# Layer 3 of a fused graph-attention kernel: the order of scores, products and small tasks rewritten in bursts of ten

## The chip, the core and the metric

The kernel runs on one core of a Trainium2 chip. The metric is the device time of one execution in microseconds (us); three runs of the kernel before had a median of 2003.11 us, from 2002.91 to 2005.37. The engines are called PE (matrix products; PEld are its weight loads), DVE (vector), ACT (activation functions), POOL and SP (which issues DMAs). Each engine works through its own instructions in order; PSUM holds what PE writes.

## What is computed

Four layers of graph attention over 16 batches (B) of 1024 nodes (N) with 64 features, all with one adjacency matrix of 1024 x 1024; after each, x becomes the layer norm of x plus the layer's output. The change touches layer 3, which is, cut to what matters:

```python
mask = graph + eye(N) > 0
h = einsum('bnc,hdc->bhnd', x, Wh)                    # 4 heads of 64
out_h = softmax(where(mask, h @ h.T, NEG)) @ h + bh   # per head
z = leaky_relu(concat_heads(out_h), 0.2)              # 256 features
h2 = einsum('bnk,dk->bnd', z, Wo)
out2 = softmax(where(mask, h2 @ h2.T, NEG)) @ h2 + bo
z2 = leaky_relu(out2, 0.2)
x = layernorm(x + layernorm(z2) * gamma + beta)
```

## The kernel before

Layers 0 to 2 end at about 650 us; the rest of the time is layer 3. It works in units. A **head unit** takes one pair of heads (n = 0, 1), one of 8 chunks k of 128 nodes and one half (h) of the other nodes: `scores` (L1332) multiplies 64-row tiles of hT into a score slot of two PSUM banks and has ACT take the exponential into a buffer e (L1340); `mask` multiplies e by the adjacency aT on DVE (L1344); `product` (L1347) multiplies e by vals in 64-column tiles and accumulates over k (L1351). A float32 product stands in the profile as two passes, so a unit has four PE rows for its scores and four for its product. A batch has 32 head units and 8 **outer units** for the second attention (L1479, L1484, L1497, L1504), which run one batch later; their masks cost DVE one more pass, which adds up the row sums (L1489).

Score slots come from `ps_s`, a ring of three (tag "s"). The small tasks that need PSUM take their slots from the same ring, through `two_banks` and `one_bank` (L680 to L690): the next one waits until the third before it has been read. The accumulators `acc0` and `acc1` take the other two banks; before, the two halves of heads alternate between them or share one. The buffers e are a ring of 11, from which z and the adjacency chunks are taken as well.

The small tasks of a batch are: `prep_x` (transposes x, pxT), `prep_h` (phT, copied to hT by ACT), `prep_sq` (squares, hsq), `shift_of` (column norms pn on PE, a maximum on DVE, a maximum over partitions on POOL, and later the shift on ACT), `prep_v` (vals); then for each pair of heads `project_T` (poT), `inverse` (the reciprocal of the row sums, which goes out to DRAM and comes back as r) and `quotient`; then `h_2T` (ph2T), `h_2v` (ph2v), and after the outer units `gather` (po2) and ten steps of layer norms, most on DVE.

The order is written out by hand. `run(plan)` (L1950 on) goes through 8 **bursts** a batch of five, five, five, five, three, three, three and three head units, with two outer units put into each of the last four. A burst issues all its scores; then the tasks listed under `mids`; then the products of the burst before (`drain`); then its own masks; then the tasks listed under `slots`. The engines PE, ACT, DVE and POOL keep that order. So PE alternates between five scores (64 rows by 128 columns of the array, 64*128 in the profile) and five products (128*64), with mids between them.

Of the kernel before, what the change touches and what calls it, by code (L numbers as in the profile page):

```python
# [582 lines left out]
def fast_path(  # L583
# [669 lines left out]
    def nodes_adj(c):  # L1253
        a_sb = l3.tile([P, N], I32, tag="e", name=f"adj3_{c}", bufs=11)
        nc.sync.dma_start(a_sb, adj_v[c])

        def convert():
            nc.vector.tensor_scalar(
                aN[:, c, :].rearrange("p (k q) -> p k q", q=P), a_sb.rearrange("p (q k) -> p k q", k=C),
                0.0, None, ALU.is_gt,  # L1260
            )
            own = aN[:, c, c * P : (c + 1) * P]
            nc.vector.tensor_tensor(own, own, ident16, ALU.max)

        return convert
    xT2, hTs, shifts, vals, zs, zTs = {}, {}, {}, {}, {}, {}

    def shift_of(key, sq):
# [3 lines left out]
        for c in range(n):  # L1272
            nc.tensor.matmul(
                pn[:, 2 * c : 2 * c + 2], sq[:, c * P : (c + 1) * P], pair_ones, start=True, stop=True
            )
        top = small.tile([P, 1], F32, tag="top", name="top")
        nc.vector.tensor_reduce(top, pn[:, : 2 * n], AX.X, ALU.max)  # L1277
# [49 lines left out]
    def heads(b, n):  # L1327
        held = {}

        def scores(k, h):  # L1330
# [8 lines left out]
            e = l3.tile([P, 2, HALF], F32, tag="e", name="e", bufs=11)  # L1339
# [7 lines left out]
        def product(k, h, e):  # L1347
            if k == 0:
                held[h] = ps_h.tile([P, HALF], F32, tag=f"acc{h * (1 - n)}", name=f"y_{b}_{n}_{h}")
# [49 lines left out]
        def project(q):  # L1399

            if q == 0:
                zs[b] = l3.tile([P, C, P], F32, tag="e", name=f"z_{b}", bufs=11)
# [30 lines left out]
    BURSTS, LAST = 8, 5  # L1433

    def prep_out(b):
# [7 lines left out]
        def h_2T():  # L1443
# [13 lines left out]
            nc.scalar.activation(sq, hT[:, 0, :], AF.Square)  # L1457
            nc.vector.tensor_copy(hT[:D, 1, :], hT[D:, 0, :])
# [10 lines left out]
        return z_T, h_2T, h_2v  # L1469

    def head_out(b):
        held = {}

        def scores(k):
# [8 lines left out]
            e = l3.tile([P, 2, HALF], F32, tag="e", name="e", bufs=11)  # L1483
# [357 lines left out]
    slots, mids = {}, {}  # L1841
# [4 lines left out]
    def at(b, j, task, where=slots):  # L1846
        where.setdefault((b, j), []).append(task)

    for c in range(C):
        convert = {}  # L1850
        at(0, c, lambda c=c, convert=convert: convert.update(go=nodes_adj(c)))
        at((c + 1) // BURSTS, (c + 1) % BURSTS, lambda convert=convert: convert["go"]())
    for b in range(B):
        z_T, h_2T, h_2v = outs[b][0]
        chain = [
            *work[b][0][1], *work[b][1][1], *([z_T] if b == E else []), h_2T,
            lambda b=b: shift_of(b, hTs[b][1]), h_2v,
        ]
        ends = outs[b][1][1]

        places = [(5, mids), (5, mids), (5, slots), (9, mids), (9, mids), (9, slots), (10, mids), (11, mids), (12, mids)]
        places += [(18, mids), *((j, slots) for j in (18, 19, 19, 20, 22, 24, 24, 24, 25, 28))]
        if b == E - 2:
            places[9:] = [(17, mids), *((j, slots) for j in (17, 17, 18, 18, 20, 20, 21, 22, 22, 24))]
        elif b == E - 1:
            places[9:] = [(j, slots) for j in (15, 15, 15, 15, 15, 17, 17, 17, 18, 18)]
        elif b == E:
            places[3] = 7, mids
            places[4:] = [(j, slots) for j in [7] * 5 + [10] * 11]
        for task, (j, where) in zip(chain + ends, places):  # L1870
            t = min(j // BURSTS, E - b)
            at(b + t, j - t * BURSTS, task, where)


    ended = slots[E, BURSTS - 1]
    slots[E, BURSTS - 1] = [ended[i] for i in (5, 0, 1, 6, 2, 3, 7, 8, 9, 4)]
    rest = slots[E, BURSTS + 2]
    slots[E, BURSTS + 2] = [*rest[2:4], rest[0], *rest[4:7], rest[1], *rest[7:]]
# [166 lines left out]
```

## Time and profile before

| | |
|---|---|
| median of three runs | 2003.11 us |
| the profiled execution | 2005.96 us |
| its span, first to last instruction | 2003.7 us |
| granted PE clock, mean | 0.981 |
| first score of layer 3 | 650.0 us |
| first score of batch 4, of batch 14 | 959.4, 1772.7 us |
| last score (outer units of batch 15) | 1969.0 us |

The page of the profile lists per engine busy time, share of the span and number of instructions; then groups of instructions with the source line, engine, operation, what is written and read, shapes, count, busy time, mean length, and the idle time before them with who ended it. A timeline lists start, length and group in order of time. In a span of consecutive batches the pattern repeats every two batches, since preparation is done for two batches at once.

### The profile page before, as it was taken

What the parts mean: (1) busy time and instruction counts of PE and PEld (TensorE: products, weight loads), DVE (VectorE), ACT (ScalarE), POOL (GpSimd) and SP (SyncE); (2) the same over time, 40 slices, a digit from 0 to 9 for tenths busy, and PEclk for the clock granted to TensorE, in tenths of its full rate; (3) what the DMA queues carried; (4) which work ended last, traced back from release to release, by engine and by line L of the source; (5) the groups of instructions that cost most, each with busy time, mean ns of one, the idle gap of its engine ahead of it and who ended that gap; (6) DMA issues with size and microseconds to landing.
All of it is one profiled execution on the core that took longest, in us unless ns stands there. A gap on an engine that the chain in (4) does not pass through costs nothing.

```text
span 2003.7 us, 25793 instructions
## 1 busy us (share of the span) xinstructions
PE 1891.7 (94%) x9545; PEld 768.3 (38%) x9545; DVE 1764.4 (88%) x2930; ACT 1333.4 (67%) x2343; POOL 81.9 (4%) x77
## 2 busy tenths in 40 slices
PE   7999989998888999999999999999999999999985
PEld 3444447763332333333333333333333333333322
DVE  5899988879999868798898899989989899889996
ACT  5356567767776766676767766766677676776543
POOL 0000000000000000000000000000000000000001
PEclk8999989999999999999999999999999999999997
DMA  7000000000000210000000000000000000100000
GB/s 175 1 1 1 1 1 1 1 1 1 1 1 11 66 31 12 12 22 17 12 17 27 12 17 12 20 26 12 17 12 27 17 12 17 28 12 17 11 17 18
DMA packets 45603, 35.89 MB, mean 18 GB/s; under 512 B 37279, under 2 KB 37344, under 8 KB 45470
## 3 DMA queue, kind: packets, MB, share of 16 engines
q1 hardware_dynamic: 45166, 34.14, 6.6%
q8 instruction: 77, 1.26, 0.3%
q14 instruction: 56, 0.46, 0.1%
q10 hardware_dynamic: 304, 0.03, 0.0%
HBM read 29.45 MB, written 4.70 MB: 17 GB/s over the span
## 4 chain that ended last, share of the span: by engine, by line
PE 61%; DVE 24%; ACT 11%; issue 3%; DMA 1%; POOL 0%; SPq 0%; POOLq 0%; DVEq 0%; ACTq 0%
PE y L1351 16%; PE s L1336 14%; DVE e L1344 8%; DVE e L991 7%; PE y_l L1003 6%; PE po L1776 5%; ACT e L1340 5%; PE y L1504 4%; PE u_l L1015 3%; PE s L1479 3%; ACT e L1484 2%; PE ph2T L1452 1%; PE phT L1310 1%; PE poT L1378 1%; ACT x L780 1%
## 5 line engine op out<-in xcount | busy, mean ns | idle before, releaser
L1340 ACT ACTIVATE e<-s,shift 128x1024 f32<-128x1024 f32 x512 | 542.6, 1119 | 320.1 <-PE s L1336 320.0
L1344 DVE TENSOR_TENSOR e<-e,aT 128x1024 f32<-128x1024 f32 x512 | 599.0, 1215 | 14.8 <-ACT e L1340 14.6
L1351 PE MATMUL y<-e,vals 128*64 128x512 f32 x2048 | 494.0, 605 | 12.5 <-ACT yT L1358 5.9
L1336 PE MATMUL s<-hT 64*128 64x512 f32 x2048 | 497.3, 605 | 1.4 <-ACT e L1340 0.9
L991 DVE SCALAR_TENSOR_TENSOR e<-G_l,q,aT 128x1024 f32<-128x1024 f32 x256 | 315.3, 1275 | 3.9 <-ACT G_l L968 3.9
L1336 PEld LDWEIGHTS s<-hT 64*128 64x128 f32 x2048 | 186.3, 186 | 290.4 <-issue 153.3
L1003 PE MATMUL y_l<-e,vals_l 128*64 128x512 f32 x1024 | 254.2, 616 | 26.9 <-DVE e L991 20.1
L1351 PEld LDWEIGHTS y<-e,vals 128*64 128x64 f32 x2048 | 135.9, 137 | 303.8 <-issue 205.0
L1497 DVE TENSOR_TENSOR e<-e,aT 128x1024 f32<-128x1024 f32 x128 | 156.3, 1225 | 10.4 <-ACT e L1484 1.0
L1489 DVE SCALAR_TENSOR_TENSOR junk<-e,aN 128x1024 bf16<-128x1024 f32 x120 | 146.1, 1217 | 0.0
L1484 ACT ACTIVATE e<-s,shift 128x1024 f32<-128x1024 f32 x128 | 142.0, 1116 | 0.2 <-PE s L1479 0.2
L1504 PE MATMUL y<-e,h2v 128*64 128x512 f32 x512 | 131.6, 597 | 0.6 <-DVE e L1497 0.6
L1479 PE MATMUL s<-h2T 64*128 64x512 f32 x512 | 130.7, 591 | 0.0
L1003 PEld LDWEIGHTS y_l<-e,vals_l 128*64 128x64 f32 x1024 | 62.3, 138 | 160.4 <-issue 75.7
L1776 PE MATMUL po<-hi,aR 128*128 128x512 f32 x256 | 102.7, 402 | 11.2 <-ACT hi L1705 7.3
L1279 POOL PARTITION_ALL_REDUCE gtop<-top x48 | 55.1, 1148 | 1302.0 <-DVE top L1277 996.5
L1776 PE MATMUL po<-lo,aR 128*128 128x512 f32 x256 | 101.1, 396 | 0.0
L780 ACT ACTIVATE x<-m,bn_shift,bn_rstd 128x64 f32<-128x64 f32 x256 | 88.5, 430 | 0.0
L1479 PEld LDWEIGHTS s<-h2T 64*128 64x128 f32 x512 | 49.9, 186 | 60.0 <-issue 26.2
L1383 ACT COPY zT<-poT 64x512 f32<-64x512 f32 x124 | 71.9, 580 | 1.3 <-PE poT L1378 0.2
L1504 PEld LDWEIGHTS y<-e,h2v 128*64 128x64 f32 x512 | 36.5, 137 | 76.0 <-issue 54.0
L978 ACT ACTIVATE vals_l<-x,p 128x64 f32<-128x64 f32 (+1 forms) x256 | 64.3, 339 | 0.0
(252 smaller groups left out, 1874.9 us busy)
## 6 DMA issues: line engine op xcount, KB each, us to landing
r<-inverse SPq DMA_DIRECT2D x62, 256.0 KB
adj<-in_adj_dram SPq DMA_DIRECT2D x16, 512.0 KB
x<-in_x_dram SPq DMA_DIRECT2D x16, 256.0 KB
out_dram<-res SPq DMA_DIRECT2D x16, 256.0 KB
rows<-yT SPq DMA_DIRECT2D x62, 4.0 KB
sums<-rows SPq DMA_DIRECT2D x31, 8.0 KB
inverse<-rt SPq DMA_DIRECT2D x31, 8.0 KB
wl<-in_L_gnn_Wh_dram SPq DMA_DIRECT2D x2, 64.0 KB
```

The costliest lines, as they stand in the source:

```text
L991: nc.vector.scalar_tensor_tensor(e, G[b - b % 2][:, b % 2, :], pq[b - b % 2][1][:, k, b % 2 : b % 2 + 1], aT[:, k, :], ALU.max, ALU.mult,)
L1003: nc.tensor.matmul(held["y"][h * D : (h + 1) * D, :], vals[b][:, k, :], e[:, h * HALF : (h + 1) * HALF], start=(k == 0), stop=(k == C - 1),)
L1336: nc.tensor.matmul(s[:, i, :], hT[rows, k * P : (k + 1) * P], hT[rows, cols], start=True, stop=True)
L1340: nc.scalar.activation(e, s, AF.Exp, bias=shifts[b, n])
L1344: nc.vector.tensor_tensor(e, e, bc_mid(aT[:, k, h * HALF : (h + 1) * HALF], 2), ALU.mult)
L1351: nc.tensor.matmul(held[h][i * D : (i + 1) * D, :], vals[b][:, k, :], e[:, i, :], start=(k == 0), stop=(k == C - 1),)
L1479: nc.tensor.matmul(s[:, i, :], hT[rows, (i + k // CH) % 2, k % CH * P : (k % CH + 1) * P], hT[rows, 0, :], start=True, stop=True,)
L1484: nc.scalar.activation(e, s, AF.Exp, bias=shifts[b])
L1489: nc.vector.scalar_tensor_tensor(junk.rearrange("p c q -> p (c q)").bitcast(BF16), e.rearrange("p i q -> p (i q)"), 1.0, aN[:, k, :], ALU. ...
L1497: nc.vector.tensor_tensor(e, e, aT[:, k, :].rearrange("p (i q) -> p i q", i=2), ALU.mult)
L1504: nc.tensor.matmul(held["o"][h * D : (h + 1) * D, :], vals["out", b][:, k, :], e[:, h, :], start=(k == 0), stop=(k == C - 1),)
L1776: nc.tensor.matmul(po.rearrange("p q k f -> p (q k f)"), aR[:, k, ic * P : (ic + 1) * P], e[:, k].rearrange("p q k f -> p (q k f)"), start ...
```

## The change

It reorders layer 3; what is computed stays. The order of the built program's instructions shows the following.

- A batch has 4 bursts (Q) of eight head units, one (n, h) each, and two outer units after them, of an earlier batch. Scores are issued in the order heads, outer; masks likewise.
- Products are issued in the same burst, after the MID tasks, and the last two (KEPT, the outer units') stay back until the products of the next burst. So PE issues ten scores, MID tasks, two kept products, eight head products, END tasks. From the seventh burst on, the PE order repeats every eight bursts: `8+2 scores, poT, 10 products, ph2v, phT` / `scores, pn, pn, po2, products, phT` / `scores, poT, products, phT` / `scores, pn, pn, ph2T, products, pn` / `scores, poT, products, ph2v` / `scores, pxT, po2, products` / `scores, poT, products` / `scores, ph2T, products, pn, phT`.
- Tasks have three places in a burst, TOP (before the scores), MID (after the masks of the first six units; PE's part stands after all the scores) and END, with an order number. `phT` and `ph2v` stand at END, between products and scores; `poT` and `ph2T` at MID. Two `hsq` tasks per two batches stand at TOP, ahead of the exponentials of that burst.
- Deferred steps (`catch_up`: shifts, and steps of the roots) come after the first four scores and at the burst's end.
- `shift_of` for the outer attention copies the norms from PSUM with ACT first; `h_2T`'s two copies on DVE become a task of their own, `swap`.
- Head products always accumulate in `acc0`. The ring e has 12 buffers; z uses the buffer of xT, the adjacency chunks the buffer of zT, two chunks of 512 KB at a time, four times, each loaded after the conversion of the ones before.
- The last batch has two bursts of the usual kind and three of eight with outer units mixed in, then the outer units of batch 15 in 5 and 3 as before.

The diff, cut to its core:

```diff
-        a_sb = l3.tile([P, N], I32, tag="e", name=f"adj3_{c}", bufs=11)
-        nc.sync.dma_start(a_sb, adj_v[c])
-
-        def convert():
+        a_sb = l3.tile([P, 2, N], I32, tag="zT", name=f"adj3_{c}", bufs=1)
+        for i in range(2):
+            nc.sync.dma_start(a_sb[:, i, :], adj_v[c + i])
...
+        norms = pn[:, : 2 * n]
+        if copied:
+            norms = small.tile([P, 2 * n], F32, tag="norms", name="norms", bufs=1)
+            nc.scalar.copy(norms, pn[:, : 2 * n])
         top = small.tile([P, 1], F32, tag="top", name="top")
-        nc.vector.tensor_reduce(top, pn[:, : 2 * n], AX.X, ALU.max)
+        nc.vector.tensor_reduce(top, norms, AX.X, ALU.max)
...
-            e = l3.tile([P, 2, HALF], F32, tag="e", name="e", bufs=11)
+            e = l3.tile([P, 2, HALF], F32, tag="e", name="e", bufs=12)
...
-                held[h] = ps_h.tile([P, HALF], F32, tag=f"acc{h * (1 - n)}", name=f"y_{b}_{n}_{h}")
+                held[h] = ps_h.tile([P, HALF], F32, tag="acc0", name=f"y_{b}_{n}_{h}")
...
-                zs[b] = l3.tile([P, C, P], F32, tag="e", name=f"z_{b}", bufs=11)
+                zs[b] = l3a.tile([P, C, P], F32, tag="xT", name=f"z_{b}", bufs=1)
...
-    BURSTS, LAST = 8, 5
+    Q, KEPT, LAST = 4, 2, 5
...
+    TOP, MID, END = range(3)
+
+    def at(burst, place, task, order=5):
+        table.setdefault((burst, place), []).append((order, len(table.get((burst, place), [])), task))
+
+    for c in range(0, C, 2):
+        convert = []
+        load, go = [(0, TOP), (0, MID), (0, END), (1, MID)][c // 2], [(0, MID), (0, END), (1, MID), (1, END)][c // 2]
+        at(*load, lambda c=c, convert=convert: convert.extend(nodes_adj(c)), 6)
+        for i in range(2):
+            at(*go, lambda i=i, convert=convert: convert[i](), 4)
...
+        places = ((2, MID, 3), (2, MID, 4), (2, END, 5)) if b < E else ((2, END, 3), (3, TOP, 4), (3, END, 5))
+        for task, (j, place, order) in zip(first, places):
+            at(g + j, place, task, order)
...
+                [*second, h_2T, swap, lambda b=b: shift_of(b, hTs[b][1], True), h_2v],
+                ((4, MID, 3), (4, MID, 4), (4, END, 5), (5, MID, 8), (5, END, 1), (5, END, 2), (6, MID if b == E - 1 else END, 8)),
...
+            (11, MID), (11, END), (11, END), (12, TOP), (12, TOP), (13, TOP), (13, TOP), (13, MID), (14, TOP), (14, TOP),
+            (15, TOP),
...
+            (-5, MID, 0, lambda b=b: prep_x(b)),
+            (-3, END, 9, lambda b=b: prep_h(b, 0, 0)), (-2, MID, 6, lambda b=b: prep_sq(b, 0, 0)),
+            (-2, END, 9, lambda b=b: prep_h(b, 0, 1)), (-1, TOP, 6, lambda b=b: prep_sq(b, 0, 1)),
+            (-2, END, 6, lambda b=b: prep_v(b)),
+            (-1, MID, 0, lambda b=b: shift_of((b, 0), hTs[b, 0][1])),
+            (-1, MID, 0, lambda b=b: shift_of((b + 1, 0), hTs[b + 1, 0][1])),
+            (-1, END, 9, lambda b=b: prep_h(b, 1, 0)), (0, MID, 6, lambda b=b: prep_sq(b, 1, 0)),
+            (0, END, 9, lambda b=b: prep_h(b, 1, 1)), (1, TOP, 6, lambda b=b: prep_sq(b, 1, 1)),
+            (1, MID, 0, lambda b=b: shift_of((b, 1), hTs[b, 1][1])),
+            (1, MID, 0, lambda b=b: shift_of((b + 1, 1), hTs[b + 1, 1][1])),
+            (2, END, 6, lambda b=b: prep_v(b + 1)),
...
-        for j in range(BURSTS):
-            n = 5 if j < 4 else 3
-            burst, units = units[:n], units[n:]
-            if j >= 4:
-                for i, unit in enumerate(outer[2 * (j - 4) : 2 * (j - 3)]):
-                    burst.insert(1 + 2 * i, unit)
-            plan.append((b, j, burst))
+        for q in range(Q if b < E else 2):
+            outer = outs[(Q * b + q - 6) // Q][1][0] if Q * b + q >= 6 else []
+            o = (Q * b + q - 6) % Q * 2
+            burst = units[q * C : (q + 1) * C] + outer[o : o + 2]
+            if (b, q) == (E, 1):
+                burst = [burst[i] for i in (0, 1, 2, 3, 8, 4, 5, 9, 6, 7)]
+            plan.append((burst, 4, KEPT if len(burst) > C else 0))
+    heads_last, outer_last = work[E][1][0][:], outs[E - 1][1][0][:]
+    for kinds, kept in (("hhhhohho", KEPT), ("ohhohhho", KEPT), ("hohohohh", 0)):
+        plan.append(([(heads_last if kind == "h" else outer_last).pop(0) for kind in kinds], 4, kept))
...
-        for b, j, burst in plan:
+        for burst, (units, soonest, kept) in enumerate(plan):
+            tasks(burst, TOP)
+            if burst == 0:
+                catch_up()
+            made = []
+            for i, unit in enumerate(units):
+                if i == soonest:
+                    catch_up()
+                made.append((unit, unit[0]()))
+
+            def masked(some):
+                for (_, mask, product), e in some:
+                    mask(e)
+                    waiting.append(lambda product=product, e=e: product(e))
+
+            cut = min(6, len(units))
+            masked(made[:cut])
+            if soonest >= len(units):
+                catch_up()
+            tasks(burst, MID)
+            masked(made[cut:])
+            while len(waiting) > kept:
+                waiting.pop(0)()
             catch_up()
-            made = [(unit, unit[0]()) for unit in burst]
-            tasks(mids, b, j)
-            while roots:
-                roots.pop(0)()
-            drain()
-            made = [(product, mask(e)) for (_, mask, product), e in made]
-            waiting.extend(lambda product=product, e=e: product(e) for product, e in made)
-            if (b, j, burst) == plan[-1]:
-                drain()
-            tasks(slots, b, j)
+            tasks(burst, END)
```

## The prediction, on record before the change was run

> **What bounds the kernel now.** I read the page's first part, then its costliest groups.
>
> ```profile
> PE 1891.7 (94%) x9545; PEld 768.3 (38%) x9545; DVE 1764.4 (88%) x2930; ACT 1333.4 (67%) x2343; POOL 81.9 (4%) x77
> ...
> L1340 ACT ACTIVATE e<-s,shift 128x1024 f32<-128x1024 f32 x512 | 542.6, 1119 | 320.1 <-PE s L1336 320.0
> L1344 DVE TENSOR_TENSOR e<-e,aT 128x1024 f32<-128x1024 f32 x512 | 599.0, 1215 | 14.8 <-ACT e L1340 14.6
> L1351 PE MATMUL y<-e,vals 128*64 128x512 f32 x2048 | 494.0, 605 | 12.5 <-ACT yT L1358 5.9
> L1336 PE MATMUL s<-hT 64*128 64x512 f32 x2048 | 497.3, 605 | 1.4 <-ACT e L1340 0.9
> ```
>
> PE is the engine that hardly idles; ACT waits 320 us for scores. The windows view over two batches of layer 3 (engines in the order PE, PEld, DVE, ACT, POOL) says the same of the stage that changes:
>
> ```profile
> 1284.00:1447.00 163.00, 160.54 (x780) 58.10 (x776) 148.43 (x196) 112.87 (x146) 7.05 (x6) 1.00 0.07 18
> ```
>
> PE 160.5 of 163 at a granted clock of 1.00, DVE 148.4, ACT 112.9. So the order of PE's work sets layer 3. Its timeline (start, length, group) gives the prices:
>
> ```profile
> 1532.49 1.08 PE L1351 MATMUL y<-e,vals 128*64 128x512 f32 x4
> 1533.40 1.03 PE L1504 MATMUL y<-e,h2v 128*64 128x512 f32 x4
> 1534.26 1.03 PE L1351 MATMUL y<-e,vals 128*64 128x512 f32 x4
> 1535.12 1.03 PE L1504 MATMUL y<-e,h2v 128*64 128x512 f32 x4
> 1535.97 1.03 PE L1351 MATMUL y<-e,vals 128*64 128x512 f32 x4
> 1536.93 4.56 PE L1336 MATMUL s<-hT 64*128 64x512 f32 x20
> 1541.43 1.09 PE L1378 MATMUL poT<-yT,wb 64*64 64x512 f32 x8
> 1542.44 4.08 PE L1351 MATMUL y<-e,vals 128*64 128x512 f32 x18
> ```
>
> Starts of products are 0.857 us apart; five products take 4.44 and five scores 4.50, so an alternation costs 8.94 where ten halves of 0.857 need 8.57: 0.36 for its two changes of array shape. A poT between them adds 1.02.
>
> Last, who releases PE when scores run long. Only the tail has a run over five; its weight loads:
>
> ```profile
> 1964.86 0.34 PEld L1479 LDWEIGHTS s<-h2T 64*128 64x128 f32 x4 [0.52 <-ACT e L1484]
> 1965.87 0.30 PEld L1479 LDWEIGHTS s<-h2T 64*128 64x128 f32 x4 [0.67 <-ACT e L1484]
> 1966.87 0.30 PEld L1479 LDWEIGHTS s<-h2T 64*128 64x128 f32 x4 [0.70 <-ACT e L1484]
> 1967.87 0.30 PEld L1479 LDWEIGHTS s<-h2T 64*128 64x128 f32 x4 [0.70 <-ACT e L1484]
> ```
>
> From the fifth score on they start 1.00 apart, each released by an exponential: the kernel has three score slots in PSUM. The same binds a task that takes a slot, here in PE's and then ACT's timeline:
>
> ```profile
> 1330.96 0.66 PE L1465 MATMUL ph2v<-ident,h2T 64*128 64x64 f32 x8
> 1331.92 0.34 PE L1273 MATMUL pn<-pair_ones,hsq 128*128 128x2 bf16 x8 [0.30 <-ACT e L1484]
> ```
>
> ```profile
> 1329.75 1.11 ACT L1340 ACTIVATE e<-s,shift 128x1024 f32<-128x1024 f32 x1
> 1330.75 1.12 ACT L1484 ACTIVATE e<-s,shift 128x1024 f32<-128x1024 f32 x1
> ```
>
> Exponentials follow each other every 1.00 us. pn is the seventh slot after five scores and ph2v, and starts 0.05 after the fourth exponential ends (1330.75 + 1.12 = 1331.87).
>
> **What the change takes off PE**, per two batches (162.7 us: the first scores of batches 4 and 14 stand at 959.4 and 1772.7, five pairs). Content is 80 units of 2 x 0.857 = 137.1, unchanged. 16 alternations become 8: 16 x 0.36 = 5.8 becomes 2.9. The rest, 162.7 - 137.1 - 5.8 = 19.8, is tasks and their waits. Laid in their new places without waits, from rows where nobody waited: four poT 1.02 each; two po2 0.53; two ph2T next to products 1.8; two ph2v 0.49 to 0.59; two double pn 0.46, two outer pn 0.2; one pxT 1.02; four phT next to scores 0.96; together 16.3. The product that waited for yT's copy (5.9 us in all) goes as well, since acc0 comes round with ten scores between. Without new waits: 137.1 + 2.9 + 16.3 = 156.3, 6.4 less than now.
>
> [...] The row says 0.36, two measured changes with their slow first passes. [...]
>
> **What it adds on PE: slot waits.** The new order is ten scores, then a task that wants one to three slots, then ten products (two kept, eight new). Count from the first score. The first exponential starts e0 = 1.18 later (1071.71 against 1070.53 in an ordinary burst), 1.08 if scores follow phT or ph2v. Exponential k (from 0) ends at e0 + 1.12 + 1.00k, and 0.05 later frees the slot for score k + 3. PE alone would reach the task at 8.77. The task's slot comes with exponential 7, at 1.18 + 8.17 = 9.35: 0.58 lost. A second slot comes at 10.35, a third at 11.35. Two pn with po2, and two pn with ph2T, need three: the third task could start at 9.23 and starts at 11.35, 2.1 lost. Queued behind it are all ten products on PE; DVE's reductions of pn and gather's multiply wait too, with four units' masks behind them. Eight products precede the one that needs mask 6, some 7 us, which covers that; uncovered, it would cost up to 2 us in each of these bursts.
>
> On top comes what ACT has before its first exponential: it now stands in the queue where ACT formerly idled. Copies follow each other at about 0.48, squares at 0.53 (1413.0 to 1415.5). Where yT, two hT and two hsq precede, the first exponential is 1.05 late; with vals and h2v as well 1.1; elsewhere 0 to 0.15. A shift after the fourth score adds 0.25 in two bursts.
>
> The eight bursts, each e0 and delay + 8.17 (10.17 with the third slot), task, ten products with their changes 8.7, tasks after them:
> 1: 9.50 + poT 1.02 + 8.73 + ph2v, phT 1.45 = 20.7
> 2: 12.35 + po2 0.53 + 8.73 + phT 0.96 = 22.6
> 3: 9.40 + 1.02 + 8.73 + 0.96 = 20.1
> 4: 12.30 + ph2T 1.77 + 8.68 + pn 0.2 = 22.95
> 5: 9.70 + 1.02 + 8.73 + 0.49 = 19.95
> 6: 9.35 + pxT 1.02 + po2 0.53 + 8.73 = 19.6
> 7: 9.35 + 1.02 + 8.73 = 19.1
> 8: 9.35 + 1.77 + 8.68 + 0.2 + 0.96 = 20.95
> Sum 166.0, 3.3 more than 162.7. Bursts 6 to 61 are seven such rounds: +23 us.
>
> [...] Were evacuation no limit the sum would be 156.3, with it 166.0.
>
> **The rest.** DVE's work stays, some 74 us a batch; in a burst it is 14.4 for masks (eight at 1.15, two outer units at 2.5 with their sum) plus 3 to 6 of tasks, 18 to 20 against 19 to 23 of PE, so it is hidden; it becomes the bound if PE's burst falls to 19. Sixteen norms copies cost about 0.2 each on ACT (nearest row ln_rstd, 0.21), hidden but for the queue above, and free pn's slot without DVE; at most 3 us. The 12 e buffers hold ten new and two kept units. The rows, sums, inverse and r transfers keep about 9 us from yT to its reciprocal and 7.5 from there to the quotient, where the trace used 4 and 6.5 to 9; SP has nothing else in layer 3 but out and adj. POOL's reductions (1.15) end before the fourth score of the next burst.
>
> Adjacency loads now share one buffer, 1 MB at a time, each behind DVE's conversion of the one before; DVE waits for the landing with masks behind it. At the 175 GB/s of the first slice 1 MB takes 6 us, of which two masks hide 2.3. Bound: 0 (a free landing) to 8 us over three loads; I take 4, as part ends under the products. The first six bursts by the same walk (eight scores) take 95.7 + 4, now 96.5 (650.0 to 746.5): +3. The tail has the same masks and chain; -5 to +5, taken as 0.
>
> Sum +26. The profiled execution took 2005.96 with a span of 2003.7; it would become 2032. The runs' median, 2003.11, is 2.9 below it; I add the 26 to that: 2029.
>
> **Rivals.** *The saved alternations win (faster).* If tasks and late scores were not held by exponentials, 7 x -6.4 + 3 = -42: 1961. If only the first slot were waited for (0.58 x 8 = 4.6), -1.8 a round: 1993. The deciding point is the wait per round: below 6.4 us, 0.8 a burst, the change gains. For it: PE is the bound, and every saved gap counts. Against: the rows above show PE released by ACT, and each burst has a task behind ten scores.
> *DVE becomes the bound (slower still).* If the waits of the reductions and gather (2 to 3 us in three bursts) add up and masks go at 1.22 instead of 1.15, DVE needs 148.4 + 9.9 of forced idling + 6.7 = 165, and with idling at each burst's start up to 169.5: +47 in seven rounds, 2053. Against: DVE has 6 us before a product needs its mask.
> *The start costs more.* Loads wait in full and the masks never catch up in batch 0: +8 on the forecast, 2037.
>
> **Chances.** Slot waits as summed 0.64 (2029, between 2005 and 2045 as delays vanish or grow), DVE 0.14, only part of the waits 0.12 (1985 to 2005), the full gain 0.06, start 0.04. The range of 1996 to 2056 leaves out the full gain, half the part case and a little above. A measurement of this kernel tells 0.2% (4 us) from no change: faster 0.16, same 0.06, slower 0.78.
>
> **What would show it.** In the new profile: scores from the seventh of a burst 1.00 apart and released by ACT; the PE task after them 9.4 us after the first score, ph2T or po2 behind two pn at 11.4 or later; rounds of about 166 us with PE's busy share lower than now; the gap of an alternation still 0.36. Wrong if PE's scores run at 0.857 throughout, if products wait for DVE's masks in most bursts, or if a round is under 162.

## The result, and the profile after

The changed kernel takes 2025.17 us (median of 4 runs, 2024.17 to 2029.57), the kernel before 2003.01 us beside it: a ratio of 1.0113, 95% interval 1.0095 to 1.013. It is slower. The profiled execution took 2024.17 us with a span of 2022.4, 18.7 more than before's 2003.7.

The page of the changed kernel, its first part and its three costliest groups:

```profile
PE 1908.8 (94%) x9545; PEld 758.6 (38%) x9545; DVE 1766.1 (87%) x2930; ACT 1327.4 (66%) x2359; POOL 53.1 (3%) x77
...
L1350 DVE TENSOR_TENSOR e<-e,aT 128x1024 f32<-128x1024 f32 x512 | 590.5, 1214 | 66.7 <-ACT e L1346 66.7
L1346 ACT ACTIVATE e<-s,shift 128x1024 f32<-128x1024 f32 x512 | 524.7, 1137 | 15.0 <-PE s L1342 11.1
L1342 PE MATMUL s<-hT 64*128 64x512 f32 x2048 | 491.4, 615 | 13.2 <-ACT e L1346 11.9
```

The first thing to see is what does not show. PE looks as busy as before, and its scores wait only 11.9 us. What turned is where ACT idles: its exponentials waited 320 us for scores and now wait 11.1. The masks, which waited 14.6, wait 66.7 us for exponentials. ACT still has time to spare (it was busy for 67% of the span before and is for 66% now), but in another place. The waits views, before and then after, show it in front of yT, the copy that follows the last product of an accumulator:

```profile
ACT yT L1358 <- PE y L1351: 27.4, 32, 3.1
...
ACT yT L1364 <- PE y L1357: 363.2, 61, 8.7
```

So ACT works without a break while PE computes ten scores, and idles while PE computes ten products. PE's own wait stands with its weight loads, in the waits view of that engine:

```profile
PEld s L1342 <- ACT e L1346: 213.2, 316, 2.9
...
PEld s L1488 <- ACT e L1346: 80.1, 115, 0.7
```

Before, the same view had for the head scores:

```profile
PEld s L1336 <- ACT e L1340: 55.2, 130, 1.8
...
PEld s L1336 <- ACT e L1484: 28.3, 60, 0.5
```

PE's matmuls themselves idled 11.9 us for exponentials, so these totals are not lost time; what is lost shows in the lengths of the runs of scores. PE's timeline of the changed kernel, one burst and the head of the next (start, length, group, wait):

```profile
1289.60 7.51 PE L1342 MATMUL s<-hT 64*128 64x512 f32 x32
1296.99 2.13 PE L1488 MATMUL s<-h2T 64*128 64x512 f32 x8
1299.05 1.09 PE L1384 MATMUL poT<-yT,wb 64*64 64x512 f32 x8
1300.07 1.94 PE L1513 MATMUL y<-e,h2v 128*64 128x512 f32 x8
1301.84 7.04 PE L1357 MATMUL y<-e,vals 128*64 128x512 f32 x32
1308.80 1.13 PE L1316 MATMUL phT<-xT,whT 64*128 64x512 f32 x4
1309.77 2.74 PE L1342 MATMUL s<-hT 64*128 64x512 f32 x12
1313.16 5.15 PE L1342 MATMUL s<-hT 64*128 64x512 f32 x20 [0.65 <-ACT e L1346]
...
1320.25 0.35 PE L1275 MATMUL pn<-pair_ones,hsq 128*128 128x2 bf16 x8
1321.20 0.34 PE L1275 MATMUL pn<-pair_ones,hsq 128*128 128x2 bf16 x8 [0.59 <-ACT e L1493]
1321.47 1.94 PE L1458 MATMUL ph2T<-zT,woT 128*64 128x512 f32 x8
```

In the first burst the ten scores take 9.45 (1289.60 to 1299.05), the ten products with the change of shape behind them 8.73 (1300.07 to 1308.80). In the second, where two squares stand on ACT ahead of the exponentials, the ten scores take 10.48, then two norms wait for slots, and the first product follows at 1323.23, 13.46 after the first score. Over one round of eight bursts the windows view reads (PE, PEld, DVE, ACT, POOL, clock):

```profile
1289.60:1454.70 165.10, 162.49 (x780) 56.67 (x778) 148.55 (x195) 112.10 (x149) 2.84 (x6) 1.00 0.06 17
```

The same work of DVE and ACT, at the same clock of 1.00, now takes 165.1 us where it took 162.7. Seven such rounds would make 17 of the span's 18.7 us, but the difference is spread otherwise. Between milestones of the two traces it came as follows. Bursts are numbered from 0 here, and the milestones are starts of a score: the first of bursts 0, 6 and 62 of the changed kernel, and before, the score with as many ahead of it (the 1st, 49th and 609th).

| stretch | before | after | difference |
|---|---|---|---|
| to the first score of layer 3 | 650.0 | 653.1 | +3.1 |
| bursts 0 to 5 | 96.5 | 100.7 | +4.2 |
| bursts 6 to 61 | 1144.4 | 1151.5 | +7.1 |
| from burst 62 to the end | 112.8 | 117.1 | +4.3 |

### The profile page after: what moved, and what is told of

Read it like the earlier page. It is cut to its first block, busy times and chain, and to the rows that moved or that the text cites. A ratio compares the mean times of both kernels' runs of the same rounds, so it can differ in the third digit from the quotient of the medians.

```text
span 2022.4 us, 25879 instructions
## 1 busy us (share of the span) xinstructions
PE 1908.8 (94%) x9545; PEld 758.6 (38%) x9545; DVE 1766.1 (87%) x2930; ACT 1327.4 (66%) x2359; POOL 53.1 (3%) x77
## 4 chain that ended last, share of the span: by engine, by line
PE 67%; DVE 19%; ACT 10%; issue 3%; DMA 0%; POOL 0%; SPq 0%; POOLq 0%; DVEq 0%; ACTq 0%
PE y L1357 21%; PE s L1342 13%; DVE e L991 7%; PE y_l L1003 6%; PE y L1513 5%; DVE e L1350 5%; PE po L1785 5%; PE s L1488 5%; ACT e L1346 3%; PE u_l L1015 3%; PE poT L1384 2%; PE ph2T L1458 1%; ACT x L780 1%; PE pg L961 1%; PE ps L929 1%
## 5 line engine op out<-in xcount | busy, mean ns | idle before, releaser
L1350 DVE TENSOR_TENSOR e<-e,aT 128x1024 f32<-128x1024 f32 x512 | 590.5, 1214 | 66.7 <-ACT e L1346 66.7
L1346 ACT ACTIVATE e<-s,shift 128x1024 f32<-128x1024 f32 x512 | 524.7, 1137 | 15.0 <-PE s L1342 11.1
L1342 PE MATMUL s<-hT 64*128 64x512 f32 x2048 | 491.4, 615 | 13.2 <-ACT e L1346 11.9
L1357 PE MATMUL y<-e,vals 128*64 128x512 f32 x2048 | 455.9, 596 | 7.8 <-DVE e L1350 4.2
L1342 PEld LDWEIGHTS s<-hT 64*128 64x128 f32 x2048 | 178.2, 185 | 308.7 <-ACT e L1346 213.2
L1003 PE MATMUL y_l<-e,vals_l 128*64 128x512 f32 x1024 | 254.1, 616 | 26.9 <-DVE e L991 20.1
L1364 ACT COPY yT<-y 128x512 f32<-128x512 f32 x64 | 37.5, 586 | 367.3 <-PE y L1357 363.2
L1357 PEld LDWEIGHTS y<-e,vals 128*64 128x64 f32 x2048 | 146.1, 137 | 301.9 <-issue 245.9
L1506 DVE TENSOR_TENSOR e<-e,aT 128x1024 f32<-128x1024 f32 x128 | 156.3, 1224 | 11.6 <-ACT e L1493 1.5
L1493 ACT ACTIVATE e<-s,shift 128x1024 f32<-128x1024 f32 x128 | 139.5, 1172 | 0.9 <-PE s L1488 0.8
L1488 PE MATMUL s<-h2T 64*128 64x512 f32 x512 | 136.9, 643 | 0.2 <-ACT e L1493 0.2
L1513 PE MATMUL y<-e,h2v 128*64 128x512 f32 x512 | 123.3, 601 | 0.9 <-DVE e L1506 0.9
L1488 PEld LDWEIGHTS s<-h2T 64*128 64x128 f32 x512 | 40.0, 187 | 87.8 <-ACT e L1346 80.1
L1015 PE MATMUL u_l<-e,only 128*32 128x512 f32 x512 | 61.6, 598 | 0.0
```

The costliest lines, as they stand in the source:

```text
L1003: nc.tensor.matmul(held["y"][h * D : (h + 1) * D, :], vals[b][:, k, :], e[:, h * HALF : (h + 1) * HALF], start=(k == 0), stop=(k == C - 1),)
L1342: nc.tensor.matmul(s[:, i, :], hT[rows, k * P : (k + 1) * P], hT[rows, cols], start=True, stop=True)
L1346: nc.scalar.activation(e, s, AF.Exp, bias=shifts[b, n])
L1350: nc.vector.tensor_tensor(e, e, bc_mid(aT[:, k, h * HALF : (h + 1) * HALF], 2), ALU.mult)
L1357: nc.tensor.matmul(held[h][i * D : (i + 1) * D, :], vals[b][:, k, :], e[:, i, :], start=(k == 0), stop=(k == C - 1),)
L1488: nc.tensor.matmul(s[:, i, :], hT[rows, (i + k // CH) % 2, k % CH * P : (k % CH + 1) * P], hT[rows, 0, :], start=True, stop=True,)
```

## The experiments

Each edit is made to the changed kernel unless it says otherwise, and each ratio is to the kernel before on the same chip, to be held against 1.0113. "Round" is the length of eight steady bursts, 165.08 in the changed kernel and 162.66 before. My theory: ten scores in a row outrun ACT's exponentials, because PSUM has three slots for them, and the saved changes of shape are paid back in slot waits. The rivals: something else in the new order, above all DVE's masks or the places of the tasks, costs the time.

**1. The two kept products inside the run of scores.** They come after the fourth score, so PE has something to do while ACT catches up; this adds one alternation a burst.

```diff
             for i, unit in enumerate(units):
                 if i == soonest:
                     catch_up()
+                if i == 4:
+                    while waiting:
+                        waiting.pop(0)()
                 made.append((unit, unit[0]()))
```

> The changed kernel, with one move: the two kept products go to PE after the fourth score of a burst instead of after all ten and the MID task. Theory (slot waits: ten scores outrun ACT's exponentials and the three slots): the two products fill the time in which PE would wait, at the price of one more alternation. From the walk a plain burst loses 0.58 of wait and gains 0.36 of changes, the bursts with three slots save about 1.0 each: some 4 us per round of eight bursts, 28 us in all, to about 1997 us, and the run of scores after the fourth no longer stands 1.00 apart. Rival (PE's waits are not what the change costs, or DVE's masks are): the 56 further alternations of 0.36 add 20 us, to about 2045.

Measured: 2005.18 beside 2003.67, ratio 1.0002 (0.999 to 1.0013), round 162.08. An ordinary burst in PE's timeline:

```profile
1281.21 3.60 PE L1342 MATMUL s<-hT 64*128 64x512 f32 x16
1284.74 1.94 PE L1513 MATMUL y<-e,h2v 128*64 128x512 f32 x8
1286.61 3.70 PE L1342 MATMUL s<-hT 64*128 64x512 f32 x16
1290.14 1.95 PE L1488 MATMUL s<-h2T 64*128 64x512 f32 x8
1292.02 1.09 PE L1384 MATMUL poT<-yT,wb 64*64 64x512 f32 x8
```

Ten scores and two products take 10.81 (1281.21 to 1292.02). Twelve at 0.857 are 10.28 and an alternation 0.36, together 10.64: the scores hardly wait. No work was removed and an alternation was added, yet the time fell by 1.1%, so the length of the run of scores is what cost. The theory holds; its 1997 was too low (3.0 us a round came of the 4), since the waits behind squares and norms stayed (that kernel still has `pn` 0.59 late behind an exponential).

**2. Norms and a gather product moved behind the products.** The two `pn` that follow another slot-taking task go from MID to END, so only one or two tasks wait for slots behind ten scores.

```diff
-            (11, MID), (11, END), (11, END), (12, TOP), ...
+            (11, END), (11, END), (11, END), (12, TOP), ...
...
-            (-1, MID, 0, lambda b=b: shift_of((b + 1, 0), hTs[b + 1, 0][1])),
+            (-1, END, 0, lambda b=b: shift_of((b + 1, 0), hTs[b + 1, 0][1])),
...
-            (1, MID, 0, lambda b=b: shift_of((b + 1, 1), hTs[b + 1, 1][1])),
+            (1, END, 0, lambda b=b: shift_of((b + 1, 1), hTs[b + 1, 1][1])),
```

> The changed kernel, with three MID tasks that take score slots moved to END: the shift's norms (pn) of the odd batch, twice in a round of eight bursts, and gather's po2. The tasks cost PE the same; only the second and third slot behind ten scores are no longer asked for. Theory of slot waits: burst with pn, pn, po2 goes from 21.96 to about 21.1, the one with pn, pn, ph2T from 22.34 to about 22.0, some 1.2 us a round, 8 us in all, to about 2017 us. Rival (place of the tasks indifferent): 2025, or a little more, since the moved tasks add changes of array shape.

Measured: 2025.13 beside 2003.67, ratio 1.0098 (1.0073 to 1.0122), round 164.76. A miss: of the microsecond a round that I expected 0.3 came, and the time does not tell it from none. The burst with `po2` fell from 21.96 to 21.31, but that with `ph2T` only from 22.34 to 22.26: `ph2T` starts 11.43 after the first score, 0.27 earlier than before the edit, and the moved `pn` takes 0.22 at its new place. So the third slot was never held by the tenth exponential, as I had counted. The two bursts after a moved norm grew by 0.18, since its shift now stands between ACT's exponentials.

**3. The second half's squares on POOL.** ACT's queue ahead of the exponentials is two squares shorter in the two bursts where they stand at TOP.

```diff
-            nc.scalar.activation(sq[:, cols], hT[:, cols], AF.Square)
+            if h:
+                nc.gpsimd.tensor_tensor(sq[:, cols], hT[:, cols], hT[:, cols], ALU.mult)
+            else:
+                nc.scalar.activation(sq[:, cols], hT[:, cols], AF.Square)
```

> The changed kernel, with the two hsq squares that stand at TOP, ahead of a burst's exponentials on ACT, made by POOL instead. Theory: they delay the first exponential, and so every score from the fourth on, by 1.05 us in two bursts of eight; without them a round is 2.1 us shorter, 15 us in all, about 2010 us. If POOL is slower than ACT by more than the ten scores take (pn waits for the squares), part of it comes back. Rival (ACT's queue ahead of the exponentials is hidden): 2025.

Measured: 2014.07 beside 2003.67, ratio 1.0045 (1.0028 to 1.0063), round 163.34; the two bursts fell from 21.96 to 20.92 and from 22.34 to 21.68. PE's timeline of the second of them:

```profile
1306.51 7.50 PE L1345 MATMUL s<-hT 64*128 64x512 f32 x32
...
1315.95 0.35 PE L1275 MATMUL pn<-pair_ones,hsq 128*128 128x2 bf16 x8
1316.90 0.34 PE L1275 MATMUL pn<-pair_ones,hsq 128*128 128x2 bf16 x8 [0.59 <-ACT e L1496]
1317.56 1.94 PE L1461 MATMUL ph2T<-zT,woT 128*64 128x512 f32 x8 [0.32 <-DVE top L1283]
```

Ten scores take 9.44 here (10.48 with the squares on ACT): 1.04 less, the pitch of two squares. An engine at 66% sets PE's pace for a microsecond, because its queue order puts the squares first. A round gained 1.74 of the 2.1 expected: the last line has a new releaser, DVE's reduction, which takes 0.32 back. It returns in experiment 6.

**4. More work for DVE.** Every second outer unit is masked twice (so those entries are multiplied by the mask a second time), about 9 us of DVE a round.

```diff
-            nc.vector.tensor_tensor(e, e, aT[:, k, :].rearrange("p (i q) -> p i q", i=2), ALU.mult)
+            for _ in range(2 - k % 2):
+                nc.vector.tensor_tensor(e, e, aT[:, k, :].rearrange("p (i q) -> p i q", i=2), ALU.mult)
```

> The changed kernel with more work for DVE and none for the others: the mask of every second outer unit is applied twice (the adjacency is 0 or 1, so the values stay). That is 8 more passes of 1.2 us in a round of eight bursts, DVE goes from 148.5 to about 158 us of a round of 165.1. Theory (PE with its slot waits sets the round): 2025 us, within a few us. Rival (DVE's masks set it): 9.7 us a round, 68 us in all, about 2093.

Measured: 2035.82 beside 2005.51, ratio 1.0161 (1.0132 to 1.019). The windows view of one round:

```profile
1250.00:1415.40 165.40, 162.46 (x778) 56.65 (x776) 157.72 (x203) 112.00 (x149) 2.81 (x6) 1.00 0.07 17
```

DVE went from 148.55 to 157.72, the round from 165.1 to 165.4 (165.49 over eight bursts): of 9.2 us added, 0.4 came through (0.7 in two of the seven rounds). DVE is not the bound in steady bursts. The added work shows in the last round and the tail, which took most of the 0.5%: the last round took 166.85 (163.18 in the changed kernel), and the stretch from burst 62 to the end 120.3 instead of 117.1.

**5. Bursts of five, tasks where the change puts them.** The runs of ten are cut into five and five, with the products half a burst behind.

```diff
+                if i == 5 and burst <= Q * E:
+                    while waiting:
+                        waiting.pop(0)()
+                    if burst < Q * E:
+                        masked(made)
+                        made = []
...
-            cut = min(6, len(units))
+            cut = min(6, len(units)) - (5 if burst < Q * E else 0)
...
-            while len(waiting) > kept:
+            while len(waiting) > (len(units) - 5 if burst < Q * E else kept):
```

> The changed kernel with its places for tasks kept and the burst's length undone: every burst of batches 0 to 14 is split into five and five (or five and three) units, products half a burst behind, so that PE alternates 120 times as often as before the change in those batches instead of 60. Theory: the alternations cost 8 x 0.36 = 2.9 us more per round, the slot waits of about 10 us fall to some 4 (the third slot behind five scores, and the squares' delay), so a round takes about 163.3 instead of 165.1, 12 us less in all: about 2012 us, though it has twice the alternations. Rival (alternations are the dear part, waits are hidden): 2025 + 20 = 2045.

Measured: 2002.25 beside 2003.67, ratio 0.9989 (0.9975 to 1.0004), round 161.67 where 163.3 was expected. PE's timeline of an ordinary burst:

```profile
1234.48 4.49 PE L1342 MATMUL s<-hT 64*128 64x512 f32 x20
1238.90 2.80 PE L1357 MATMUL y<-e,vals 128*64 128x512 f32 x12
1241.53 1.89 PE L1513 MATMUL y<-e,h2v 128*64 128x512 f32 x8
1243.34 2.85 PE L1342 MATMUL s<-hT 64*128 64x512 f32 x12
```

Five scores take 4.42 (1234.48 to 1238.90) and 4.49 (1243.34 to the next task at 1247.83), as in the kernel before: no slot is waited for. The round is 1.0 below that of before, with the same number of alternations. So, as far as this run separates them, the other parts of the change gain a microsecond a round (the places of the tasks by array shape are the likely ones), and the length of ten loses 3.4, though it saves eight alternations.

**6. Experiments 1 and 3 together.** The edits are those above, unchanged.

> The two edits that gained, together: kept products after the fourth score, and the two squares at TOP on POOL. In the first alone the two bursts with these squares still have four scores in 4.45 and 4.52 us where the others take 3.53 to 3.63. Theory: that 1.9 us a round goes, from 162.1 to about 160.2, 13 us less than the first alone, about 1992 us; the two waits do not overlap, so the gains of 20 and 11 us add up to within a few us. Rival (one wait, counted twice): no better than the kept products alone, 2005.

Measured: 2009.85 beside 2005.51, ratio 1.002 (1.001 to 1.0031), rounds 161.4 to 163.1. A clear miss: instead of adding up, the second edit took back part of the first. The burst with `ph2T` grew from 21.87 (experiment 1) to between 22.1 and 23.8. PE's timeline of one that took 23.83:

```profile
1316.70 0.35 PE L1275 MATMUL pn<-pair_ones,hsq 128*128 128x2 bf16 x8
1317.64 0.34 PE L1275 MATMUL pn<-pair_ones,hsq 128*128 128x2 bf16 x8 [0.59 <-ACT e L1496]
1319.10 2.44 PE L1461 MATMUL ph2T<-zT,woT 128*64 128x512 f32 x8 [1.12 <-DVE top L1283]
1321.32 8.29 PE L1360 MATMUL y<-e,vals 128*64 128x512 f32 x32
```

and the same time in the windows view:

```profile
1316.90:1320.30 3.40, 1.69 (x21) 0.82 (x19) 3.37 (x7) 1.70 (x2) 0.72 (x2) 1.00 0.02 5
1320.30:1323.70 3.40, 3.40 (x10) 0.98 (x8) 3.37 (x5) 1.22 (x2) 0.00 (x0) 0.52 0.00 0
```

`ph2T` takes the slot of a `pn`, which DVE's reduction `top` must read first, and DVE comes late. While PE waited it was half filled (1.69 of 3.40 us), and the next 3.4 us were granted 0.52 of the clock: eight products took 8.29 instead of 7.09, ph2T 2.44 instead of 1.94. The wait of 1.1 became a loss of 2.8. In another round the same burst waits the same 1.12 (ph2T at 994.61) and keeps its clock; it takes 22.14:

```profile
992.72:996.13 3.41, 1.86 (x16) 0.88 (x17) 3.38 (x7) 1.38 (x2) 0.72 (x2) 1.00 0.02 5
996.13:999.55 3.42, 3.42 (x18) 1.15 (x16) 3.38 (x5) 1.22 (x2) 0.00 (x0) 1.00 0.00 0
```

Why DVE is late stands in its own timeline of the same burst:

```profile
1307.72 1.53 DVE L1574 TENSOR_TENSOR m<-v,ln_rstd 128x512 f32<-128x512 f32 x1
1309.29 1.41 DVE L1575 TENSOR_TENSOR m<-m,gamma 128x512 f32<-128x512 f32 x1
1310.73 0.69 DVE L1580 TENSOR_TENSOR m<-m,beta 128x512 f32<-128x512 f32 x1
...
1312.07 6.90 DVE L1353 TENSOR_TENSOR e<-e,aT 128x1024 f32<-128x1024 f32 x6
1318.88 0.25 DVE L1283 TENSOR_REDUCE top<-pn 128x1 f32<-128x16 f32 x2
```

while POOL had the two squares:

```profile
1306.84 3.31 POOL L1332 TENSOR_TENSOR hsq<-hT 128x512 bf16<-128x512 f32 x2 [28.44 <-ACT hT L1325]
```

Two operations of 0.69 took 1.53 and 1.41 beside the squares: 1.56 us lost. That leaves two readings, the squares on POOL hold DVE up, or the reduction stands behind too many masks now that PE is earlier. Experiments 7 to 11 bear on that and on what each edit is worth.

**7. Experiments 1, 2 and 3 together.** If `ph2T` need not follow a second norm, DVE's lateness should not reach PE.

> As the one before, and pn of the odd batch and po2 at END too. What waits for slots is left at two places of a round (pn, pn before po2 or ph2T: 1.2 us where 0.46 is work), so theory gives up to 1.5 us a round less some 0.4 for added changes of shape: about 0.7, 5 us in all, about 1987 us. From the run with this move alone, which gained 0.3 a round and nothing in the time, the rival says 1992 or a little more.

Measured: 1991.35 (1990.45 to 1993.4) beside 2005.51, ratio 0.9935 (0.991 to 0.996), round 159.58. PE's timeline of the `ph2T` burst, which fell to 20.88:

```profile
1307.92 0.35 PE L1275 MATMUL pn<-pair_ones,hsq 128*128 128x2 bf16 x8
1308.87 1.94 PE L1461 MATMUL ph2T<-zT,woT 128*64 128x512 f32 x8 [0.59 <-ACT e L1496]
```

One wait of 0.59 is left, none for DVE. The round is where theory put it (0.7 below the 160.2 expected of experiment 6); the time is nearer the rival's 1992 than 1987. This version is faster than both kernels, by 0.65% than the one before.

**8. Experiments 5, 2 and 3 together.** The same repair for bursts of five.

> Bursts of five with the tasks in the change's places, the TOP squares on POOL and pn and po2 at END. In the run with fives alone a round took 161.7, of which 1.9 are the squares' delay (5.45 and 5.53 us for five scores where 4.4 to 4.5 are usual) and about 1.2 waits for third slots. Theory: about 159 us a round, 19 us less than fives alone, 1984 us. Rival (DVE, with 148.5 of 161.7 busy and now behind PE by less, becomes the bound): a round of 161, no better than 1998.

Measured: 1998.96 beside 2005.51, ratio 0.997 (0.9958 to 0.9982), round 160.59. It beats the kernel before, but by less than expected. Its waits view of PE names where the rest went:

```profile
PE s L1345 <- DVE top L1283: 10.1, 7, 2.8
```

The norm that was moved to END now holds a slot that the next burst's score wants, and DVE reads it late: the `po2` burst takes 21.27, where experiment 7 has 19.92.

**9. Experiment 6 with four masks, not six, ahead of the reductions.**

```diff
-            cut = min(6, len(units))
+            cut = min(4, len(units))
```

> Kept products in the run of scores and squares on POOL, as in the sixth experiment, but only four masks, not six, stand in DVE's queue ahead of the tasks at MID and so of the norms' reductions. If ph2T waits because DVE comes late to the reduction, behind six masks that POOL's squares held up by some 1.5 us, the wait of 1.1 us and the lost clock behind it go: the burst with ph2T falls from between 22.1 and 23.8 to about 20.9, the round to about 160, ratio 0.995 to the kernel before, about 1996 us beside 2005. If the wait has another cause (POOL's own lateness, or the slot behind an exponential), the round stays at 161.4 or more and the ratio at 1.002, about 2009; if masks five and six, now behind the reductions, make products wait, it is longer still.

Measured: 2012.94 beside 2003.42, ratio 1.0044 (1.0028 to 1.0061), rounds 161.6 to 163.6. A miss, and no help in telling the readings apart: `ph2T` still waits up to 1.2 for `top`, because DVE starts its masks 8.6 us after the first score instead of 6.2, and so gives back just what two masks take. The squares now stretch two other operations of DVE (1.00 and 0.97 where they take 0.16 and 0.17 in experiment 6).

**10. Experiment 7 with the squares back on ACT** (experiments 1 and 2 together).

> The best version so far with the squares back on ACT: kept products in the run of scores, second norm and gather product at END. If the three edits are worth what each stage showed, the squares delay two bursts a round by 1.04 again and the round is about 161.3, ratio 0.997, about 1999 us beside 2005. If instead the move to END pays only where POOL made DVE late, the round stays at about 162, that of the kept products alone, ratio 1.000, about 2005.

Measured: 2002.31 beside 2003.42, ratio 0.9987 (0.9974 to 1.0), round 161.43, as theory had it. The move to END is worth 0.65 a round here, and the squares on POOL 1.85 on top. In the time, the intervals of experiments 1 and 10 overlap.

**11. Experiment 6 with the second half's squares left out.** The norms are taken of the first half twice, so the shifts rest on half of the columns. ACT's queue is as short as in experiment 6, and POOL does nothing beside DVE.

```diff
-            if h:
-                nc.gpsimd.tensor_tensor(sq[:, cols], hT[:, cols], hT[:, cols], ALU.mult)
-            else:
+            if not h:
                 nc.scalar.activation(sq[:, cols], hT[:, cols], AF.Square)
...
+        C2 = n if copied else n // 2
-                pn[:, 2 * c : 2 * c + 2], sq[:, c * P : (c + 1) * P], pair_ones, ...
+                pn[:, 2 * c : 2 * c + 2], sq[:, c % C2 * P : (c % C2 + 1) * P], pair_ones, ...
```

> Kept products in the run of scores, as in the sixth experiment, but the second half's squares are left out altogether: the norms are taken of the first half twice, so that the shifts may differ. ACT's queue is short, as with squares on POOL, but POOL does nothing beside DVE's operations of that time. If POOL's squares hold DVE up (1.53 and 1.41 us instead of 0.69) and that makes the reduction late, ph2T no longer waits 1.1 us for it: its burst takes about 21.0 us, the round about 160.4, ratio 0.995, about 1994 us beside 2004. If DVE is late only because the exponentials and so PE come earlier, the burst stays at about 22.1 or more, the round at 161.4, ratio 1.002, about 2008.

Measured: 1990.25 beside 2005.22, ratio 0.9921 (0.9895 to 0.9946), round 160.22. PE's timeline of its `ph2T` burst, which takes 20.94:

```profile
1306.67 0.35 PE L1276 MATMUL pn<-pair_ones,hsq 128*128 128x2 bf16 x8
1307.62 0.34 PE L1276 MATMUL pn<-pair_ones,hsq 128*128 128x2 bf16 x8 [0.59 <-ACT e L1495]
1307.88 1.94 PE L1460 MATMUL ph2T<-zT,woT 128*64 128x512 f32 x8
```

The wait for DVE is gone with both norms and six masks in their places. So POOL's squares made DVE late. And without them the two edits of experiment 6 do add up: 162.08 less 0.93 in each of two bursts is 160.2.

## Why the prediction was right, point by point

2029 was forecast, 2025.17 measured. The mechanism was the predicted one: ten scores outrun the exponentials, and the slot waits cost more than the saved alternations bring. That the total lies within 4 us is in part luck. Of the 26 us forecast for the span, 23 were for the steady bursts, 3 for the start and 0 for the tail; measured are 18.7, as 7.1, 7.3 and 4.3. And the medians, which the forecast is held against, lie 22.2 apart where the profiled spans lie 18.7 apart.

*The price of an alternation* held. The ten products with their changes were put at 8.73 from the row, and took 8.73 from the first to the task behind them: ten at 0.857 are 8.57, which leaves 0.16 for the one change of shape in that stretch, half of 0.36 being 0.18.

*The slot waits* held, burst by burst:

| burst of a round | 1 | 2 | 3 | 4 | 5 | 6 | 7 | 8 | sum |
|---|---|---|---|---|---|---|---|---|---|
| predicted | 20.7 | 22.6 | 20.1 | 22.95 | 19.95 | 19.6 | 19.1 | 20.95 | 166.0 |
| measured | 20.77 | 21.96 | 20.16 | 22.34 | 19.85 | 19.78 | 19.19 | 21.03 | 165.08 |

The first task of burst 3 of a round was to start 9.40 after the first score and started at 9.45 (1289.60 to 1299.05); the squares' 1.05 is 10.48 in burst 4 beside 9.43 in bursts 7 and 8. Experiments 1, 3 and 5 each removed a part of these waits, and the time fell by 20, 11 and 23 us where 28, 15 and 12 were expected. One sign named ahead did not come: PE's busy share of a round was to fall, and is 162.49 of 165.10, as before (160.54 of 163). The work is the same, so PE's rows cover most of the waits. And one sum is off: the tasks as listed add up to 16.0, not 16.3, which makes a round without waits 156.0.

*The third slot* is the term that was too large, by 0.6 in bursts 2 and 4. I let the third task wait for the tenth exponential, to 12.30. `ph2T` started 11.70 after the first score, while that exponential was still running. The weak step is that I counted slots only as ACT frees them: the first `pn` gives its own back, once DVE has reduced it, and `ph2T` takes that one. (So the ring does not always hand out the third slot before, as the description of the kernel before has it: experiment 6 shows `ph2T` released by `top`.) In the changed kernel DVE was early enough for that to be a gain; in experiment 6 it was late, and the same slot became a loss.

*Seven rounds at 3.3, +23:* measured +7.1 between bursts 6 and 62. The steady rounds are 2.4 longer, some 17 in seven; but the baseline was not seven steady rounds. The last eight bursts of the kernel before took 168.72, 6.1 more than a steady round, and I had not looked at them. PE's timeline of before shows the largest part:

```profile
1881.63 1.98 PE L1452 MATMUL ph2T<-zT,woT 128*64 128x512 f32 x4 [3.11 <-DVE zT L786]
1883.39 6.60 PE L1351 MATMUL y<-e,vals 128*64 128x512 f32 x20
```

`ph2T` waits 3.11 for DVE, and the five products after it take 6.60 instead of 4.51; that is 5.2 of the 6.1. The changed kernel has no such stall, and its own first and last rounds are 2 us shorter than its steady ones. So slot waits explain 17 of the forecast's 23; that only 7.1 of them show is due to the ends of the stretch.

*The start, +3:* measured +7.3. The loads were no issue (the longest wait for one is 1.43 us on DVE). Missed was a step that the change moves: a `phT` now stands at TOP before the first score (2.08, and 0.50 until a copy on ACT), which is most of the first 3.1; the other half microsecond to the first score lies in the layers before, which the change does not touch. In the six bursts after it (numbered from 0) a product of burst 0 waits 1.49 for its mask, behind four conversions of the adjacency, and a score in burst 3 waits 2.08 for an exponential. These do not add up to the 4.2 by themselves, since the kernel before loses time there too (2.61 us waiting for yT, and behind that a granted clock of 0.50 from 707.42 to 711.03). With bursts of five (experiment 5) the same stretch takes 97.5, so the length of the runs has a share in it.

*The tail, 0:* measured +4.3. "The same masks and chain" does not hold. Both halves of a head pair now share acc0, and with eight units a burst its copy is not hidden: products wait 0.73 and 2.81 for yT (1916.29, 1939.55). But that is not where the time went, for the kernel before has a wait there too, of 5.72 for a mask (1943.81). Up to the last head pair's `po` (1966.30 in the changed kernel, 1952.65 before) the changed kernel's tail is 0.8 shorter. From there to the first of the last eight scores it is 2.7 longer, those scores take 1.0 more, and from the issue of the last output DMA to the end it is 1.3. The windows view, the changed kernel and then before, from that `po` on:

```profile
1966.30:1969.70 3.40, 3.40 (x16) 3.40 (x16) 3.06 (x12) 0.00 (x0) 0.00 (x0) 0.50 0.00 0
...
1952.65:1956.05 3.40, 2.25 (x18) 2.02 (x19) 2.00 (x7) 0.00 (x0) 0.00 (x0) 1.00 0.00 0
```

The same work met half the clock in the changed kernel and the full clock before; the last scores, too, began at a lower clock (0.58 from 1976.50 to 1979.90). These are readings of one execution each. No run tested them, and whether the lower clock falls there in other executions is not shown.

*The rivals.* That the saved alternations win fell: against the 156.3 without waits, 8.8 us of a round were lost, more than the 6.4 below which the change would have gained. What was to be had shows in experiment 7: 156.3 and eight more alternations at 0.36 are 159.2, and its round is 159.58. That DVE becomes the bound fell in experiment 4 for the steady bursts. That the start costs more was right in sign and worth 4 of the 8 us I gave it, but not by the way I gave, full waits for the loads.

## What to carry to other kernels

Alternation is not only overhead: while PE does the other kind of work, the evacuating engine, here ACT, drains its ring. With three PSUM slots, 1.00 us an exponential and 0.857 a score, five scores ran free and ten lost 0.6 us and more a burst; two products in the middle of the run gave it back for one alternation, and the wait showed only in the weight loads' waits, in ACT's idle time, which moved from the exponentials to the copy behind the products, and in the length of a run of scores. When a repair is then moved to an idle engine, look at whose operations get longer beside it, and who releases the same slot next.

## What the runs showed of the hardware that was not expected

POOL's squares stretched operations of DVE beside them, though neither waits for the other in these rows: 0.69 us became 1.53 and 1.41 (experiment 6), 0.16 and 0.17 became 1.00 and 0.97 (experiment 9). Without the squares (experiment 11) the same four take 0.69, 0.69, 0.16 and 0.17. What the two engines share there, no run shows. The price here was 1.56 us of DVE's time in a burst. Through the late `top` and the lost clock that became 1.2 to 2.9 us of a burst: between the profiled runs of experiments 6 and 11, 12.2 of 17.8 us lie in the bursts with `ph2T` (ratios 1.002 and 0.9921).

PE lost a part of its clock behind a stretch in which it was half filled: in experiment 6, 3.40 us with 1.69 of PE work were followed by 3.40 us at a granted clock of 0.52 and the next 3.40 at 0.98, while the same burst of another round, with 1.86 of work in 3.41 us, kept 1.00. What decides between the two is not shown.

The first score of layer 3 moved from run to run, from 652.3 (experiment 4) to 662.9 (experiment 8) in kernels that differ from each other only behind it or just ahead of it. The five kernels with squares on POOL lie at 655.7 to 662.9, the others at 652.3 to 656.0; some of those squares run just ahead of the first score, so a part of the spread may be theirs. So a single span cannot settle a few microseconds here; the lengths of rounds can.
